# Deformable layer: one of eight corner products of a tap moved from ScalarE to GpSimd, behind a later tap's gathers

## The chip, the cores and the metric

The kernel runs on one core of one Trainium2 chip. The metric is the device time of one execution in microseconds (us), and the median of three runs stands for a kernel. The engines go by the names of the profile: PE is TensorE's matmul (PEld its weight load), DVE is VectorE, ACT is ScalarE, POOL is GpSimd, SP is SyncE, which here issues every transfer but the gathers.

## The reference

The input x has four images of 128 channels and 128 x 128 pixels. Each image goes through four layers, each a normalisation over groups of channels, a convolution of some kind and a residual sum. Layer 0, the one that matters here, is a deformable convolution. A 3 x 3 convolution gives, for each pixel and each of the nine taps, an offset in y and x and a mask. Each tap then reads the image at its own shifted, fractional position, by bilinear interpolation of the four pixels around it, and a 128 x 128 product with the tap's weights sums the nine taps:

```python
def corner(yi, xi, wgt):
    valid = (yi >= 0) & (yi < H) & (xi >= 0) & (xi < W)
    idx = jnp.clip(yi, 0, H - 1) * W + jnp.clip(xi, 0, W - 1)
    v = jax.vmap(lambda xb, ib: jnp.take(xb.reshape(C, H * W), ib, axis=1))(x, idx)
    return v * (wgt * valid)[:, None]
return corner(y0i, x0i, (1 - ly) * (1 - lx)) + corner(y0i, x0i + 1, (1 - ly) * lx) \
    + corner(y0i + 1, x0i, ly * (1 - lx)) + corner(y0i + 1, x0i + 1, ly * lx)
...
sampled = _bilinear_sample(x, py, px) * mask[:, None]
return jnp.einsum('bckhw,ock->bohw', sampled, weight.reshape(weight.shape[0], C, KK))
```

Layer 1 is a 5 x 7 dilated convolution. Layer 2 is a selective state-space block: its core is a scan with 16 states a channel over the pixels in four directions. Layer 3 is a 3 x 3 difference convolution.

## The kernel before

An image is cut into 32 blocks of four rows (512 pixels). In layer 0 a unit of work is a tap of a block: 32 x 9 = 288 taps an image, 1152 in all. Ahead of it, `layer0_table` writes the normalised image into a table in memory, in which one row holds the four pixels around a position, 4 x 128 numbers, so that one gathered row brings all that the interpolation of one output pixel needs. `positions` works out offsets, masks, indices (`idx`) and weights (`wt` for the two upper neighbours, a product in PSUM, `wl`, for the two lower ones) for strips of 16 rows.

A tap then goes through these steps:

- `gather` (L447): GpSimd issues four indirect DMAs, one for each row of the block, each of 128 table rows of 2 KB. Two rows share a tile `g` of 128 x (2 rows, 4 neighbours, 128 channels); so a tap has two tiles, h = 0 and h = 1. The partition is the pixel's column.
- `weigh_upper(h)` (L460): ScalarE multiplies the two upper neighbours of each of the tile's two rows by a column of `wt`, one instruction of 128 x 128 each, in place. That is four products a tile and eight a tap.
- `weigh_lower(h)` (L473): VectorE multiplies the lower neighbours of the tile's two rows by `wl`, one instruction of 128 x 512 a tile.
- `turn` (L484): TensorE transposes the 4 x 4 pieces and sums the four neighbours in PSUM, 16 matmuls with `ident`.
- `copy` (L496): ScalarE copies the 128 x 512 result out of PSUM into `smp`.
- `project` (L504): TensorE multiplies `smp` by the tap's weights and sums over the nine taps in `acc`.
- `add` (L511): after the ninth tap VectorE adds the residual.

The tiles of `g` come from a pool of `pairs` buffers: 20 for the first image, which is ten taps, and 10 for the others, which is five. A gather that needs a buffer waits until TensorE's `turn` of the tap that had it is done.

The order of instructions on each engine is the order in which the program writes them, and `keep_order` holds the compiler to it. `weave` sets that order: at step t it calls each stage of a list with the tap t minus the stage's delay, group after group.

```python
order = [[(2, weigh_upper(0)), (2, weigh_lower(0)), (3, turn), (5, project)], [(6, add), (0, gather), (4, copy(True))],
         [(2, weigh_upper(1)), (2, weigh_lower(1))], [(0, look), (3, copy(False))], []]
```

So at step t the gathers of tap t are written after the first half's products of tap t - 2 and before its second half's products. `look` advances `positions` of the next strip.

Layer 0 of the first image runs by itself. From then on `scan`, the core of layer 2, is the main work (`together`): after each step of the scan the program pulls pieces of side work, and layer 0 of the next image is a part of that. So layer 0 of images two, three and four is written between the scan's instructions. While it runs, `on_vector` gives the scan's two large products (L930, `inputs`, and L997, `outputs`) to VectorE and leaves on GpSimd only one product of 128 x 512 for each of the scan's blocks (L902), beside the gathers. VectorE also runs the scans themselves (L1073), for which ScalarE makes the decays (L960, `pa`), and TensorE spreads inputs (L923) and sums outputs (L971).

Of the kernel before, what the change touches and what calls it, by code (L numbers as in the profile page):

```python
# [13 lines left out]
AF = mybir.ActivationFunctionType  # L14
ALU = mybir.AluOpType
# [9 lines left out]
NBLK = H // R  # L25
KK = 9
# [86 lines left out]
def conv_preact_kernel(ctx: ExitStack, tc: tile.TileContext, a: dict, nb: int):  # L113
    nc = tc.nc
# [8 lines left out]
    def load(pool, src, shape, name, **kw):  # L123
        t = pool.tile(shape, F32, name=name, **kw)
        nc.sync.dma_start(t, src)
        return t
# [75 lines left out]
    def blk(t, i):  # L202
        return t[:, i * N : (i + 1) * N]
# [108 lines left out]
    def layer0(st, pairs=10):  # L312
# [5 lines left out]
        with ExitStack() as s:  # L318
# [8 lines left out]
            got = {}  # L327
# [106 lines left out]
            def where(n):  # L434
                i, k = divmod(n, KK)
                return i, k, i // BPS, i % BPS

            def gather(n):
                i, k, j, q = where(n)
                if k == 0:  # L440
                    got["x", i] = load(pp, blk(xb, i), [P, N], "xres", bufs=2)
                idx = got["i", j][1]
                for h in range(2):
                    got["g", n, h] = g = gp.tile([P, 2, 4, P], F32, name="g")
                    for r in range(2):
                        m = ((2 * h + r) * BPS + q) * KK + k
                        nc.gpsimd.indirect_dma_start(  # L447
                            out=g[:, r].rearrange("p q c -> p (q c)"),
                            out_offset=None,
                            in_=table,  # L450
                            in_offset=bass.IndirectOffsetOnAxis(ap=idx[:, m : m + 1], axis=0),
                        )

            def weigh_upper(h):
                def one(n):
                    i, k, j, q = where(n)
                    wv, g = got["i", j][0], got["g", n, h]
                    for r in range(2):
                        for c in range(2):
                            nc.scalar.activation(  # L460
                                g[:, r, c, :], g[:, r, c, :], AF.Copy, scale=wv[:, 2 * h + r, q, k, c : c + 1]
                            )

                return one

# [72 lines left out]
            for n, _ in enumerate(positions(0)):  # L538
                yield share * min(1.0, (n + 1) / 21)
            order = [[(2, weigh_upper(0)), (2, weigh_lower(0)), (3, turn), (5, project)], [(6, add), (0, gather), (4, copy(True))],  # L540
                     [(2, weigh_upper(1)), (2, weigh_lower(1))], [(0, look), (3, copy(False))], []]
            while st["rows"] <= NBLK:
# [841 lines left out]
    def head(b):  # L1384
        st = sts[b]
        table = [(loads(None, layer0_table(st), True), 12)] if b < 2 else []
        return table + [(loads("POOL", layer0(st)), 28), (loads("PE", layer1(st), True), 14),
                (loads("PE", layer2_pre(st), True), 36)]
# [11 lines left out]
    for f in layer0(sts[0], 20):  # L1400
        tick()
        for _ in range(3):
            next(ahead, None)
            tick()
# [103 lines left out]
```

## Time and profile before

| | us |
|---|---|
| median of three runs | 20858.84 (20851.53 to 20882.21) |
| the profiled execution | 20873.01 |
| its span, first to last instruction | 20871.2 |
| mean granted TensorE clock | 0.886 |

The profile is of one execution. Its times are in microseconds unless marked ns. A group's line gives the line of the kernel, the engine, the operation, tiles written and read, shapes, how many there are, busy time and mean ns of one, and then the engine's idle time just ahead of them with what ended it. The groups of layer 0's steps and of the scan's two large products:

| line | engine, what | count | busy us | mean ns |
|---|---|---|---|---|
| L447 | POOL, gathers | 4608 | 4807.6 | 1043 |
| L460 | ACT, upper neighbours | 9216 | 2897.4 | 392 |
| L473 | DVE, lower neighbours | 2304 | 1485.7 | 671 |
| L484 | PE, transposing matmuls | 18432 | 2693.6 | 303 |
| L496 | ACT, copies of PE's result | 1152 | 664.7 | 577 |
| L504 | PE, tap weights | 2304 | 1355.3 | 670 |
| L902 | POOL, 128x512 product of the scan's blocks | 512 | 652.9 | 1275 |
| L997 | DVE, 128x2048 product | 356 | 816.6 | 2294 |
| L997 | POOL, 128x2048 product | 1692 | 7670.8 | 4534 |

Idle time of an engine costs nothing unless others wait for it. "remote", or "another core or an unknown queue", marks a wait for which the profile names no instruction that ended it. "issue" is time in which the engine waited for nothing that the profile shows. A windows view gives the busy time of each engine in given stretches of the span. The chain of waits starts from what ended last and goes back, at each step, to what released it.

### The profile page before, as it was taken

How to read it: one execution, taken by the hardware profiler on the slowest of the kernel's cores; microseconds unless marked ns; L12 is line 12 of the kernel's file. 1: busy time of each engine (PE TensorE's matmuls, PEld its weight loads, DVE VectorE, ACT ScalarE, POOL GpSimd, SP SyncE). 2: the span in 40 equal slices, each digit the busy share in tenths (PEclk: the TensorE clock that was granted, in tenths of full speed). 3: DMA queues.
4: the chain of work that ended last, by engine and by line, in shares of the span. 5: the costliest groups of instructions: out<-in, count | busy, mean ns of one | idle time of the engine just before them, and what ended most of it. 6: DMA issues, size and time to landing. Idle time of an engine off the chain costs nothing.

```text
span 20871.2 us, 208527 instructions
## 1 busy us (share of the span) xinstructions
PE 15906.6 (76%) x58778; PEld 6786.0 (33%) x58778; DVE 16828.5 (81%) x14665; ACT 13184.7 (63%) x26230; POOL 15930.9 (76%) x9453
## 2 busy tenths in 40 slices
PE   4667776777878888777788887877777877677778
PEld 2444222444322223344422222344432222222223
DVE  1222588888999999878799889978889998999983
ACT  3444566677666666666667776666666767655563
POOL 3664577666788888777668888866768889999994
PEclk7878888889989999889889999988888988899899
DMA  7666678777767777777777796777776777555673
GB/s 234 191 193 190 193 228 284 248 255 252 246 206 226 231 237 254 236 253 255 247 232 226 224 249 230 255 240 246 252 237 218 235 215 220 185 185 193 199 219 120
DMA packets 2909344, 4717.42 MB, mean 226 GB/s; under 512 B 1095248, under 2 KB 1369240, under 8 KB 2831264
## 3 DMA queue, kind: packets, MB, share of 16 engines
q1 hardware_dynamic: 2539552, 3495.83, 52.3%
q0 software_dynamic: 368640, 1208.25, 18.5%
q8 instruction: 476, 7.80, 0.1%
q14 instruction: 676, 5.54, 0.1%
HBM read 3766.27 MB, written 908.60 MB: 224 GB/s over the span
## 4 chain that ended last, share of the span: by engine, by line
DVE 35%; PE 21%; issue 11%; ACT 11%; DMA 9%; another core or an unknown queue 5%; POOL 3%; SPq 3%; DVEq 0%; POOLq 0%; ACTq 0%
DVE h L1073 20%; DVE h L930 11%; PE pst L484 5%; PE psum L895 4%; DMA du<-stepsd 3%; ACT pa L960 3%; ACT g L460 3%; PE acc L504 2%; DVE g L473 2%; PE dub L923 2%; DMA delta<-stepsd 2%; PE yacc L971 2%; PE p L1303 1%; DMA g<-table,idx 1%
## 5 line engine op out<-in xcount | busy, mean ns | idle before, releaser
L1073 DVE TENSOR_TENSOR_SCAN h<-pa,carry,h 128x512 f32<-128x512 f32 x8192 | 10010.0, 1268 | 811.5 <-ACT pa L960 582.9
L960 ACT ACTIVATE pa<-delta,neg_a 128x512 f32<-128x512 f32 x8192 | 5535.9, 686 | 4528.0 <-DVE h L1073 3464.9
L997 POOL TENSOR_TENSOR h<-h,cb 128x2048 f32<-128x2048 f32 x1692 | 7670.8, 4534 | 136.3 <-POOL carry L991 0.4
L447 POOL DMA_INDIRECT g<-table,idx x4608 | 4807.6, 1043 | 2454.1 <-issue 1523.6
L930 DVE TENSOR_TENSOR h<-du,dub 128x2048 f32<-128x2048 f32 x1625 | 3688.0, 2270 | 961.8 <-PE dub L923 294.7
L484 PE MATMUL pst<-ident,g 128*128 128x128 f32 x18432 | 2693.6, 303 | 1242.6 <-issue 516.0
L923 PE MATMUL dub<-u,xb_sb 128*128 128x512 f32 x3250 | 2073.1, 724 | 1843.3 <-DVE h L930 1532.3
L484 PEld LDWEIGHTS pst<-ident,g 128*128 128x128 f32 x18432 | 2377.9, 158 | 2230.3 <-issue 1139.0
L460 ACT ACTIVATE g<-g,wt 128x128 f32<-128x128 f32 x9216 | 2897.4, 392 | 50.8 <-DMA g<-table,idx 47.6
L971 PE MATMUL yacc<-h,gather_sb 128*32 128x512 f32 x16384 | 2375.6, 644 | 108.9 <-POOL h L997 63.8
L930 POOL TENSOR_TENSOR h<-du,bb 128x2048 f32<-128x2048 f32 x423 | 1927.7, 4557 | 16.5 <-DMA du<-stepsd 16.5
L496 ACT COPY smp<-pst 128x512 f32<-128x512 f32 x1152 | 664.7, 577 | 1749.8 <-remote 1175.9
L473 DVE TENSOR_TENSOR g<-g,wl 128x512 f32<-128x512 f32 x2304 | 1485.7, 671 | 194.3 <-issue 108.5
L504 PE MATMUL acc<-smp,w_sb 128*128 128x512 f32 x2304 | 1355.3, 670 | 307.7 <-DVE x L511 162.8
L923 PEld LDWEIGHTS dub<-u,xb_sb 128*128 128x128 f32 x3250 | 600.3, 213 | 3025.2 <-DVE h L930 2200.9
L902 POOL TENSOR_TENSOR steps<-steps,u 128x512 f32<-128x512 f32 x512 | 652.9, 1275 | 1095.3 <-ACT steps L899 1080.0
L1303 PE MATMUL p<-xn,w_l_sb 128*128 128x508 f32 (+2 forms) x2304 | 1148.6, 620 | 1.8 <-ACT xn L1282 1.8
L971 PEld LDWEIGHTS yacc<-h,gather_sb 128*32 128x32 f32 x16384 | 343.5, 111 | 1886.3 <-issue 1349.6
L895 PE MATMUL psum<-e,ident 128*128 128x512 f32 x1024 | 607.1, 677 | 387.7 <-ACT bc L889 348.5
L511 DVE TENSOR_TENSOR x<-acc,xres 128x512 f32<-128x512 f32 x128 | 87.5, 684 | 967.5 <-remote 500.4
L895 PE MATMUL psum<-one_e,less 128*128 128x512 f32 x1024 | 629.2, 701 | 297.3 <-ACT one_e L891 296.5
L997 DVE TENSOR_TENSOR h<-h,cb 128x2048 f32<-128x2048 f32 x356 | 816.6, 2294 | 12.1
(169 smaller groups left out, 17288.9 us busy)
## 6 DMA issues: line engine op xcount, KB each, us to landing
cb<-bcd SPq DMA_DIRECT2D x512, 1024.0 KB
delta<-stepsd SPq DMA_DIRECT2D x2048, 256.0 KB
du<-stepsd SPq DMA_DIRECT2D x2048, 256.0 KB
stepsd<-steps SPq DMA_DIRECT2D x512, 512.0 KB
table<-gt SPq DMA_DIRECT2D x512, 256.0 KB
bb<-bcd SPq DMA_DIRECT2D x512, 256.0 KB
win<-nd SPq DMA_DIRECT2D x512, 160.0 KB
g<-table,idx POOLq DMA_INDIRECT x4608
```

Of the source, the lines that this page charges most:

```text
L447: nc.gpsimd.indirect_dma_start(out=g[:, r].rearrange("p q c -> p (q c)"), out_offset=None, in_=table, in_offset=bass.IndirectOffsetOnAxis( ...
L460: nc.scalar.activation(g[:, r, c, :], g[:, r, c, :], AF.Copy, scale=wv[:, 2 * h + r, q, k, c : c + 1])
L473: nc.vector.tensor_mul(g, g, wl.unsqueeze(3).to_broadcast([P, 2, 2, P]))
L484: nc.tensor.matmul(pst[:, r * P : (r + 1) * P], g[:, r % 2, q, :], ident, start=q == 0, stop=q == 3, is_transpose=True,)
L504: nc.tensor.matmul(got["a", i], w0[:, k, :], got.pop(("c", n)), start=k == 0, stop=k == KK - 1)
L895: nc.tensor.matmul(pd, sign, t, start=n == 0, stop=n == 3)
L923: nc.tensor.matmul(p, xb[:, seq[t][1], j, :], c["u"], start=True, stop=True)
L930: engine.tensor_mul(h, c["du"], b.unsqueeze(1).to_broadcast([P, NG, N]))
L960: nc.scalar.activation(pa, blocks[t]["d", g], AF.Exp, scale=neg_a[:, k, at : at + 1])
L971: nc.tensor.matmul(c["y"][g * Q : (g + 1) * Q, :], gather, c["h", j][:, g, :], start=j == 0, stop=last and not second,)
L997: engine.tensor_mul(h, h, c["cb"][:, j, :].unsqueeze(1).to_broadcast([P, NG, N]))
L1073: nc.vector.tensor_tensor_scan(o, f, o, carry[:, n : n + 1], ALU.mult, ALU.add)
```

## The change

At the end of `gather` of tap t, behind the last of its four indirect DMAs, GpSimd multiplies one upper neighbour of tap t - 2: of the second tile (h = 1), second row (r = 1), second neighbour (c = 1). ScalarE leaves that product out and keeps the other seven. The last two taps of an image have no tap two on, so ScalarE keeps all eight of them. A small function, `neighbour`, finds the piece and its weight for both engines. Nothing else differs.

```diff
                             in_offset=bass.IndirectOffsetOnAxis(ap=idx[:, m : m + 1], axis=0),
                         )
+                    if h == 1 and n >= 2:
+                        g, w = neighbour(n - 2, h, 1, 1)
+                        nc.gpsimd.tensor_scalar(g, g, w, None, ALU.mult)
+
+            def neighbour(n, h, r, c):
+                i, k, j, q = where(n)
+                return got["g", n, h][:, r, c, :], got["i", j][0][:, 2 * h + r, q, k, c : c + 1]
 
             def weigh_upper(h):
                 def one(n):
-                    i, k, j, q = where(n)
-                    wv, g = got["i", j][0], got["g", n, h]
                     for r in range(2):
                         for c in range(2):
-                            nc.scalar.activation(
-                                g[:, r, c, :], g[:, r, c, :], AF.Copy, scale=wv[:, 2 * h + r, q, k, c : c + 1]
-                            )
+                            if h == 1 and r == 1 and c == 1 and n + 2 < NBLK * KK:
+                                continue
+                            g, w = neighbour(n, h, r, c)
+                            nc.scalar.activation(g, g, AF.Copy, scale=w)
 
                 return one
```

## The prediction

> **What bounds the kernel now.** The change touches only the deformable layer, so I first looked for it in time. Of the views I read, in this order, the first is the page's first part, which shows no engine full over the span:
>
> ```profile
> PE 15906.6 (76%) x58778; PEld 6786.0 (33%) x58778; DVE 16828.5 (81%) x14665; ACT 13184.7 (63%) x26230; POOL 15930.9 (76%) x9453
> ```
>
> These are averages over unlike stages. The instructions of L447 (GpSimd's gathers) show that the layer runs four times, once an image, and one windows view gives the four stretches from first gather to last. Columns: stretch, its length, then busy us (and instructions) of PE, PEld, DVE, ACT, POOL, then clock, DMA share, GB/s.
>
> ```profile
> 215.00:1932.00 1717.00, 1026.82 (x5576) 738.58 (x5577) 431.75 (x751) 818.54 (x2541) 1091.61 (x1151) 0.79 0.64 191
> 3449.00:5327.00 1878.00, 1466.10 (x7295) 823.16 (x7295) 1624.06 (x1646) 1297.91 (x3361) 1278.10 (x1184) 0.89 0.75 251
> 8650.00:10449.00 1799.00, 1369.82 (x6976) 797.11 (x6976) 1416.08 (x1487) 1206.83 (x3207) 1267.88 (x1178) 0.88 0.76 248
> 13548.00:15368.00 1820.00, 1368.97 (x6966) 795.71 (x6967) 1415.21 (x1485) 1207.38 (x3208) 1273.85 (x1177) 0.87 0.75 245
> ```
>
> The reader is to see 7214 us, 35% of the span, in which ScalarE is busy 48%, 69%, 67% and 66%: not the fullest engine. POOL's busy time leaves something out. The timeline of POOL alone shows gathers 1.25 us apart, start to start, although each counts 0.95 us:
>
> ```profile
> 811.88 0.95 POOL L447 DMA_INDIRECT g<-table,idx  x1 [0.30 <-issue]
> 813.14 1.18 POOL L447 DMA_INDIRECT g<-table,idx  x1 [0.30 <-issue]
> 814.62 0.95 POOL L447 DMA_INDIRECT g<-table,idx  x1 [0.31 <-issue]
> 815.87 0.95 POOL L447 DMA_INDIRECT g<-table,idx  x1 [0.30 <-DVE g L473]
> ...
> 820.87 0.95 POOL L447 DMA_INDIRECT g<-table,idx  x1 [0.30 <-issue]
> 824.85 0.94 POOL L447 DMA_INDIRECT g<-table,idx  x1 [3.03 <-ACT smp L496]
> ```
>
> The 0.30 us ahead of a gather is there nearly every time (median over 4520 pairs 0.30). With 1152 x 0.30 = 346 us added, POOL is taken for 1438 of 1717, 1624 of 1878, 1614 of 1799 and 1620 of 1820 us: 84%, 86%, 90%, 89%. That leaves 279, 254, 185 and 200 us, 918 in all. A tap has four gathers, so POOL needs 5.0 us a tap at least; the taps come every 5.96, 6.52, 6.24 and 6.32 us.
>
> Next, who waits for whom in those gaps. ScalarE over the same microseconds:
>
> ```profile
> 809.74 2.45 ACT L460 ACTIVATE g<-g,wt 128x128 f32<-128x128 f32 x8
> 824.24 0.58 ACT L496 COPY smp<-pst 128x512 f32<-128x512 f32 x1 [12.04 <-remote]
> ```
>
> ScalarE's eight products take 2.45 us, far under the tap's 5.96; then it stands 12.04 us before a copy of PE's result. PE's last matmul of that copy's tap is recorded long before, yet PE's semaphore counts appear only at 824.1, 2.3 us after POOL had run out of gathers. In the first image 45 such releases of several counts at once come a median 2.07 us after POOL went idle. There POOL is also ten taps ahead of PE (its buffers' limit): turn follows landing by a median 43 us. So a round is: POOL works until its buffers are used up, goes idle some 2 to 3 us, PE's counts arrive, buffers come free. Its length is POOL's work plus a short idle; ScalarE's work lies inside it. I read POOL as the pacer in the first image, and as one of several in the other three, where DVE's scans (79% to 86% busy) run beside it.
>
> **The change, part by part.** For each tap but an image's last two, one of ScalarE's eight products moves: 286 an image, 1144 in all, ScalarE's L460 falls from 9216 to 8072.
>
> *Removed from ScalarE.* Eight take 2.45 us pipelined, so one is 0.30 us; 1144 of them 343 us of work. What of it was on the path: the chain of waits, asked for each stretch, gives "ACT g L460" 13.8%, 7.1%, 5.9% and 6.3%, that is 237 + 133 + 106 + 115 = 591 us; an eighth is 74 us. Where POOL paces, a shorter ScalarE ends nothing earlier, so I count a third: -25 us.
>
> *Added to POOL.* No 128x128 product with a column runs on POOL in this trace. From below: the one-input 128x128 select of masks.py:199 took 0.29 us. From above: two-input products took 1.275 us at 512 columns (L902) and 4.534 at 2048 (L997), 2.12 ns a column and 0.19 us fixed, so 0.46 us at 128; the farthest row, L902 itself, would be 1.27. I take 0.38, halfway between the near two, since it has one tensor input like the lower row but a scalar to fetch besides. Its neighbours matter as much:
>
> ```profile
> 9399.96 0.95 POOL L447 DMA_INDIRECT g<-table,idx  x1 [0.30 <-issue]
> 9400.93 1.27 POOL L902 TENSOR_TENSOR steps<-steps,u 128x512 f32<-128x512 f32 x1
> 9402.36 0.98 POOL L447 DMA_INDIRECT g<-table,idx  x1 [0.16 <-PE acc L504]
> ```
>
> A product behind a gather starts 0.02 us after it, and the next gather 0.16 us after the product. So the product costs 0.38 + 0.02 + 0.16 - 0.30 = 0.26 us of POOL's time (0.17 to 0.34 by the bounds): 74 us an image, 297 in all (194 to 389).
>
> *How much of it shows.* First image: all 74, since a round is POOL's work plus an idle that the change does not touch. Other three: POOL is taken 86% to 90%, rounds of the same kind but partly set by scans; I take two thirds of 223, 149 us. Together +223; if the idle 918 us covered it, nothing.
>
> *The new waits.* The product waits on POOL for the landing of a gather two taps back. Landing takes a median 3.7 us from issue, 7.4 at 95% and 10.1 at most; two taps back lies at least 5.0 us of gathers before. Behind a late one are queued the next tap's gathers, but POOL's instructions are accepted well before they run (at 815.5 a wait for the gather of 824.85 was already under way), so I cost it nothing; uncovered, a few tens of us. TensorE's turn waits for the product too, and VectorE's product of the lower half (L473), which today waits for ScalarE each time; the two touch interleaved rows of one tile. Today L473 of the second half starts a median 13.8, 5.3, 3.1 and 2.4 us after the end of the gathers two taps on, behind which the product will stand. Less than 0.8 us it is in 21%, 5%, 25% and 27% of the taps; in the last three images the shortfall is 0.09, 0.55 and 0.67 us a tap, 375 us if each counted. In the first image VectorE is 25% busy and it costs nothing. In the others a shortfall is a tap in which POOL is late, which the 149 us already has; I add none, and keep the 375 for a rival.
>
> *Moved past.* On POOL the product stands behind the fourth gather of its tap and ahead of the next tap's first; no DMA moves, SP's queue is untouched. L902, which feeds the scan, can stand 0.38 us later: 84 of them in these stretches, 32 us at most, within the range.
>
> **Sum.** +223 - 25 = +198 on the profiled execution's 20873.0 (span 20871.2 and 1.8 around it): 21071. The median of the three runs, 20858.8, is 14.2 lower, so 21057.
>
> **A rule weighed.** VectorE's two-input 128x2048 product stops POOL:
>
> ```profile
> 9221.97 2.29 DVE L997 TENSOR_TENSOR h<-h,cb 128x2048 f32<-128x2048 f32 x1
> 9222.25 2.84 POOL L447 DMA_INDIRECT g<-table,idx  x1 [0.30 <-issue]
> ```
>
> All 294 gathers of over 1.3 us overlap an L997, and none of the 84 L902 on POOL does. The Trainium skill (SBUF — State Buffer, Who interferes with whom) says that a VectorE instruction with two SBUF inputs blocks a GpSimd instruction that reads SBUF, but not one that only writes, descriptor generation included. The first half agrees with the L902 rows, the second does not agree with the 2.84 us gather. By the rule the products would be stopped on top of what is seen now; by the row POOL is stopped once by each L997 already, whichever instruction is next.
>
> **Rivals.**
> *The idle hides it (faster).* POOL fills its 918 us and the ScalarE share of the chain shrinks: -74, 20785. For it: in the last three images the chain gives POOL's gathers under 3% and ScalarE's products about 6%. Against: the idle comes after POOL's work, not beside it. Chance 0.24.
> *VectorE is held (slower, far).* Where VectorE catches up with POOL it stands for the product, and the scans behind it stand too. It decides once POOL's lead over VectorE falls under the product's 0.4 us, which a quarter of the taps of images three and four are near. All 297 and half of 375: +485, 21344. Chance 0.15.
> *Products stopped besides.* 334 L997 of 2.29 us in 5497 us: a product of 0.38 meets one in 16%, for some 1.15 us; 858 x 0.19 = 160 more, 21217. This is what that rule of the Trainium skill would make. For it: L902's rows; against: the stopped gathers. Chance 0.08.
> *The break frees PE's counts.* If the pause between gathers lets them through, the first image's 279 us of idle go, +74 stays: -205, 20654. Against: today's 0.30 us pauses, and L902's 1.27 us, release few. Chance 0.06.
> Forecast, POOL paces: 0.47, own range 20900 to 21190.
>
> **From cases to numbers.** 0.2% is 42 us, about what a measurement of this kernel can tell from no change. Faster: most of the first rival and the last, 0.25. Same: tails of forecast and first rival, 0.12. Slower 0.63. From 20740 to 21340 leaves out the last rival and half of the held one, some 0.15.
>
> **What would show it.** Right: the four stretches grow by about 74 and three times 50 us; POOL's new row is near 0.38 us, x1144, with gaps of 0.02 and 0.16; its idle stays near 918. Wrong: the idle shrinks by 297 and the stretches do not grow; or L473 waits for POOL in large sums; or a product of 0.6 us and more; or ScalarE's long waits for PE's counts grow rarer.

## The result and the profile after

The kernel after takes 20837.52 us (median of 18 runs, 20814.37 to 20856.60), the kernel before, measured beside it, 20880.28 us (18 runs, 20851.53 to 20901.91). The ratio is 0.9981, with a 95% interval from 0.9974 to 0.9988: **0.19% faster**, 43 us, where 0.9% slower was forecast. The profiled execution took 20838.75 us, its span 20837.0.

One thing must be said of the condition of these runs, since no later number can be understood without it: in this comparison PE's semaphore counts, by which it tells the other engines that a matmul is done, are recorded late and in bursts, as in the 12.04 us "remote" wait that the prediction shows, while in six of the eight groups of runs below they are on time and the same kernel before takes some 20,090 us.

The four stretches of layer 0 after the change, first gather to last, with columns as in the prediction's windows view (stretch, length, busy us of PE, PEld, DVE, ACT, POOL, clock, DMA share, GB/s):

```profile
217.00:1930.00 1713.00, 1048.80 (x5578) 748.18 (x5579) 434.35 (x751) 740.46 (x2264) 1288.72 (x1438) 0.80 0.64 191
3446.00:5309.00 1863.00, 1434.60 (x7314) 805.93 (x7313) 1645.09 (x1654) 1227.41 (x3092) 1540.28 (x1470) 0.90 0.78 254
8625.00:10444.00 1819.00, 1356.92 (x7011) 772.64 (x7011) 1439.83 (x1497) 1147.39 (x2946) 1489.62 (x1464) 0.90 0.76 246
13536.00:15357.00 1821.00, 1373.55 (x7011) 781.71 (x7011) 1436.60 (x1500) 1147.43 (x2946) 1490.43 (x1464) 0.89 0.76 246
```

The lengths make 7216 us; before they made 7214. POOL's busy time rose by 898 us, ScalarE's fell by 268, and the stretches did not move. The page's groups, with line numbers shifted (L460 became L468), give the cost:

```profile
L447 POOL DMA_INDIRECT g<-table,idx x4608 | 4874.2, 1058 | 1679.5 <-issue 1136.4
...
L468 ACT ACTIVATE g<-g,wt 128x128 f32<-128x128 f32 x8072 | 2577.6, 392 | 216.7 <-DMA g<-table,idx 162.4
...
L455 POOL TENSOR_SCALAR g<-g,wt 128x128 f32<-128x128 f32 x1144 | 833.0, 728 | 37.4
```

The product is far longer than the 0.38 us forecast: 0.728 us in the mean, 0.624 in the median. POOL's timeline shows how it stands between gathers, once where the buffers are used up in the first image, once in the third:

```profile
821.10 0.95 POOL L447 DMA_INDIRECT g<-table,idx  x1 [0.30 <-issue]
822.08 0.62 POOL L455 TENSOR_SCALAR g<-g,wt 128x128 f32<-128x128 f32 x1
824.79 1.05 POOL L447 DMA_INDIRECT g<-table,idx  x1 [2.09 <-issue]
...
9398.72 0.95 POOL L447 DMA_INDIRECT g<-table,idx  x1 [0.30 <-issue]
9399.70 0.76 POOL L455 TENSOR_SCALAR g<-g,wt 128x128 f32<-128x128 f32 x1
9400.64 1.01 POOL L447 DMA_INDIRECT g<-table,idx  x1 [0.17 <-issue]
```

In the median it starts 0.03 us after the fourth gather, the next gather follows 0.17 us behind it, and that gather takes 1.01 us instead of 0.95. So a product costs POOL 0.62 + 0.03 + 0.17 + 0.06 - 0.30 = **0.58 us** a tap, against 0.26 in the forecast. With 0.30 us added for each of 866 gathers and 0.20 for each of 286 products in a stretch (317 us), POOL is taken for all but 107, 6, 12 and 14 us: its idle is 139 us, where it was 918. The work did not make the stretches longer; it filled the idle.

### The profile page after: what moved, and what is told of

The parts are those of the page before. It is cut to its first block, busy times and chain, and to the rows that moved or that the text cites. A ratio compares the mean times of both kernels' runs of the same rounds, so it can differ in the third digit from the quotient of the medians.

```text
span 20837.0 us, 209864 instructions
## 1 busy us (share of the span) xinstructions
PE 15847.0 (76%) x58778; PEld 6719.5 (32%) x58778; DVE 16855.7 (81%) x14665; ACT 12887.2 (62%) x25086; POOL 16827.5 (81%) x10597
## 4 chain that ended last, share of the span: by engine, by line
DVE 34%; PE 19%; issue 12%; DMA 11%; ACT 10%; POOL 8%; another core or an unknown queue 3%; SPq 2%; DVEq 0%; POOLq 0%; ACTq 0%
DVE h L1079 20%; DVE h L936 11%; PE pst L490 4%; PE psum L901 4%; POOL g L447 3%; DMA du<-stepsd 3%; ACT pa L966 3%; DMA g<-table,idx 2%; PE acc L510 2%; ACT g L468 2%; DMA delta<-stepsd 2%; PE p L1309 1%; POOL h L1003 1%; PE yacc L977 1%
## 5 line engine op out<-in xcount | busy, mean ns | idle before, releaser
L1003 POOL TENSOR_TENSOR h<-h,cb 128x2048 f32<-128x2048 f32 x1692 | 7670.5, 4533 | 137.0 <-POOL carry L997 0.6
L447 POOL DMA_INDIRECT g<-table,idx x4608 | 4874.2, 1058 | 1679.5 <-issue 1136.4
L490 PEld LDWEIGHTS pst<-ident,g 128*128 128x128 f32 x18432 | 2312.0, 155 | 2699.8 <-issue 1297.6
L468 ACT ACTIVATE g<-g,wt 128x128 f32<-128x128 f32 x8072 | 2577.6, 392 | 216.7 <-DMA g<-table,idx 162.4
L479 DVE TENSOR_TENSOR g<-g,wl 128x512 f32<-128x512 f32 x2304 | 1488.2, 669 | 359.9 <-DMA g<-table,idx 315.4
L455 POOL TENSOR_SCALAR g<-g,wt 128x128 f32<-128x128 f32 x1144 | 833.0, 728 | 37.4
```

Source lines behind the costliest of these rows:

```text
L447: nc.gpsimd.indirect_dma_start(out=g[:, r].rearrange("p q c -> p (q c)"), out_offset=None, in_=table, in_offset=bass.IndirectOffsetOnAxis( ...
L468: nc.scalar.activation(g, g, AF.Copy, scale=w)
L479: nc.vector.tensor_mul(g, g, wl.unsqueeze(3).to_broadcast([P, 2, 2, P]))
L490: nc.tensor.matmul(pst[:, r * P : (r + 1) * P], g[:, r % 2, q, :], ident, start=q == 0, stop=q == 3, is_transpose=True,)
L1003: engine.tensor_mul(h, h, c["cb"][:, j, :].unsqueeze(1).to_broadcast([P, NG, N]))
```

## The experiments

Eight groups of runs were made; in a group each kernel is compared with the kernel before on one chip. Each kernel has one trace in its group, and whether counts are late was read from it: by ScalarE's waits "ACT smp <- remote", and by stalls, spans of over 2 us between two recorded counts of PE in which at least two of its matmuls that count have their recorded ends; a stall's length is the time from the last such end to the next count. In the kernels with ScalarE relieved and no real product on GpSimd (e1, e3, g1, h3) one upper neighbour goes unweighted into the sum.

| group | counts | before, us | kernels |
|---|---|---|---|
| first comparison | late | 20880.28 | after |
| 1 | on time | 20088.11 | e1, e2, e3, e4 |
| 2 | on time | 20108.61 | c0, c1, c2, c3 |
| 3 | on time | 20091.91 | d1 |
| 4 | on time | 20098.10 | d2 |
| 5 | late | 20863.10 | f1, f2 |
| 6 | on time | 20092.19 | g1, g2, g3 |
| 7 | on time | 20085.07 | h1 |
| 8 | late | 20879.30 | h2, h3 |

### The two halves of the change, each alone, and a doubled one

e1 is the kernel after without GpSimd's product; ScalarE keeps seven. e2 is the kernel before, ScalarE with all eight, and a product of the same size on a tile of its own (`scratch`, by a column of -1) in the product's place. e3 is the kernel after with that scratch product instead of the real one, so that nobody waits for it. e4 gives GpSimd two products a tap and ScalarE six.

e1, against the kernel after:

```diff
-                    if h == 1 and n >= 2:
-                        g, w = neighbour(n - 2, h, 1, 1)
-                        nc.gpsimd.tensor_scalar(g, g, w, None, ALU.mult)
```

e2, against the kernel before (e3 has the same product, against the kernel after, in place of the real one):

```diff
+                    if h == 1 and n >= 2:
+                        nc.gpsimd.tensor_scalar(scratch, scratch, minus, None, ALU.mult)
```

e4, against the kernel after:

```diff
-                        g, w = neighbour(n - 2, h, 1, 1)
-                        nc.gpsimd.tensor_scalar(g, g, w, None, ALU.mult)
+                        for c in range(2):
+                            g, w = neighbour(n - 2, h, 1, c)
+                            nc.gpsimd.tensor_scalar(g, g, w, None, ALU.mult)
...
-                            if h == 1 and r == 1 and c == 1 and n + 2 < NBLK * KK:
+                            if h == 1 and r == 1 and n + 2 < NBLK * KK:
```

> The eighth product is left out: ScalarE does seven, GpSimd none, so one upper neighbour goes into the sum unweighted. Theory S (slack: GpSimd's idle time before the change was spare, and ScalarE's product is a small part of the path): 0.2 to 0.5% faster than before, 20780 to 20840 us, since an eighth of ScalarE's 591 us on the chain is 74 us at most. Theory C (cancel: both engines are on the path, the changed kernel gains much on ScalarE and pays much on GpSimd): 1 to 3% faster, 20250 to 20670 us. The forecast's theory (GpSimd paces): within 0.1%, since a shorter ScalarE ends nothing earlier.

> ScalarE does all eight products as before; GpSimd does a product of the same size on a scratch tile at the same place, with no data of the tap. Theory S: within 0.3% of before (20820 to 20940), GpSimd's idle in images two to four falls from some 200 us to under 30 us each. Theory C: 1 to 3% slower (21090 to 21500). GpSimd paces: 1144 products of 0.57 us are 650 us, 21400 to 21530.

> ScalarE does seven, GpSimd a product of the same size on a scratch tile: the changed kernel's work on each engine without the wait of TensorE on GpSimd (the eighth neighbour stays unweighted). In the changed kernel TensorE's turns wait some 500 us for GpSimd's product. If that wait costs, this run is faster than the changed kernel by 0.2% or more (under 20800); if it only takes the place of waits for ScalarE and transfers, both are the same within 0.1% (20820 to 20860). Theory C expects the same as the changed kernel, 20840.

> Two of the eight products on GpSimd (both neighbours of the second tile's second row), six on ScalarE. Theory S: GpSimd is already full in images two to four (5 to 11 us idle), so each tap there pays the second product in full: 858 x 0.6 to 0.7 us = 510 to 600 us, and image one, with 98 us idle, pays some 65 us: 21400 to 21500. Theory C: the second product gains on ScalarE what it costs on GpSimd: within 0.3% of the changed kernel.

| kernel | us | ratio to before (95%) |
|---|---|---|
| e1, ScalarE relieved | 20071.31 | 0.9991 (0.9982 to 1.0000) |
| e2, GpSimd loaded | 20710.61 | 1.0304 (1.0290 to 1.0318) |
| e3, both, nobody waits | 20692.30 | 1.0300 (1.0286 to 1.0314) |
| e4, two products | 21336.07 | 1.0623 (1.0607 to 1.0639) |

Here the product is no gain but 3% of the kernel, and two are 6.2%. The kernel before was 790 us faster than in the first comparison. Either these kernels differ from the change in something not yet seen, or the group differs.

### The same two kernels once more, and a break without work

c0 is the kernel before, c1 the kernel after, both unedited, and c2 is e2 again. c3 puts a memset of one column into the kernel before, in the place of the product:

```diff
+                    if h == 1 and n >= 2:
+                        nc.gpsimd.memset(tiny, 0.0)
```

> The kernel before, unchanged, for a profile beside the others of its group. The first group's chip ran it in 20088 us, the chip of the first comparison in 20880. Theory H (held counts): the 790 us lie in the four stretches of layer 0, and a chip's time goes with how many of PE's counts appear late in bursts there: near 20090 with none, near 20880 with some 200. Theory K (another cause, such as slower transfers or a lower clock): the stretches outside layer 0 differ as well.

> The changed kernel, unchanged. On a chip without late counts GpSimd paces: 3.0% slower than before, 20680 to 20720 us, since the same work with a scratch tile took 20692 and 20711. On a chip with late counts: 0.1 to 0.3% faster than before, some 20840, as in the first comparison. If it is 0.2% faster on a chip whose before takes 20090, the data wait of the scratch runs was misread.

> ScalarE eight products, GpSimd one besides on a scratch tile. Where counts come late: GpSimd's 1144 products fill the idle that the late counts leave, so within 0.3% of before, about 20850 to 20940; if instead ScalarE's relief made the changed kernel's gain, it is slower than the changed kernel by 74 us or more. Where they don't: 3% slower, 20710.

> ScalarE eight products; GpSimd only clears one column of 128 x 1 behind each tap's gathers (some 0.1 us). If any other instruction between the gathers lets PE's counts through, a chip with late counts gains up to 600 us or so (20200 to 20400). If the counts need a pause in the gathers, or GpSimd's work only fills idle time, it stays within 0.3% of before there. Where no counts come late: 0 to 0.4% slower, 1144 x 0.04 us = 46.

c0 took 20102.89 us (0.9998, 0.9989 to 1.0008), c1 **20690.66 (1.0293, 1.0279 to 1.0307)**, c2 20717.45 (1.0302, 1.0287 to 1.0318), c3 20106.66 (1.0002, 0.9993 to 1.0011). So it is the group: the very kernel that gained 0.19% loses 2.9% where counts are on time. The first and third image of c0, the kernel before with counts on time:

```profile
217.00:1663.00 1446.00, 1001.89 (x5693) 660.76 (x5694) 483.30 (x762) 912.76 (x2597) 1091.99 (x1152) 0.92 0.76 227
...
8227.00:9875.00 1648.00, 1323.36 (x7016) 772.88 (x7016) 1433.49 (x1497) 1222.91 (x3226) 1293.87 (x1178) 0.91 0.83 272
```

POOL's busy 1091.99 and 346 us of gaps fill 1438 of 1446 us: no idle is left. Its timeline in the first image is gather after gather, 1.25 us apart, without the 3 us holes of the prediction's fence:

```profile
1007.85 0.95 POOL L447 DMA_INDIRECT g<-table,idx  x1 [0.30 <-issue]
1009.10 0.95 POOL L447 DMA_INDIRECT g<-table,idx  x1 [0.30 <-issue]
1010.36 0.95 POOL L447 DMA_INDIRECT g<-table,idx  x1 [0.30 <-issue]
```

The same two images of c1, the kernel after:

```profile
218.00:1832.00 1614.00, 1023.03 (x5671) 680.16 (x5671) 483.66 (x763) 801.18 (x2313) 1292.28 (x1438) 0.90 0.69 203
...
8512.00:10319.00 1807.00, 1360.95 (x7007) 770.38 (x7008) 1437.05 (x1497) 1151.38 (x2945) 1483.59 (x1463) 0.90 0.77 248
```

The first grows by 168 us, 0.587 a tap, and the third by 159, 0.556: close to the 0.58 us that the timeline gave for a product. All four stretches go from 6486 to 7079 us, +593, where the medians of c1 and c0 lie 588 apart. The waits of c1, with columns of sum, count and longest in us, show PE now standing for the product:

```profile
PEld pst L490 <- POOL g L455: 1829.7, 838, 7.8
PE pst L490 <- POOL g L455: 1626.7, 815, 7.4
```

Yet e3, in which nobody waits for it, costs as much (1.0300 against 1.0293). The price is POOL's time, not the wait. The memset of c3 takes 0.118 us of POOL and costs nothing: it fits into the 0.30 us that stand ahead of a gather anyway, and the gathers on either side of it start 1.25 us apart as before.

### Less work on POOL: a shorter product, and none of L902

d1 is the kernel before with L902 given to VectorE while layer 0 runs beside the scan:

```diff
-            nc.gpsimd.tensor_mul(du, delta, u)
+            (nc.vector if early else nc.gpsimd).tensor_mul(du, delta, u)
```

d2 is e2 with 48 of 128 columns:

```diff
-                        nc.gpsimd.tensor_scalar(scratch, scratch, minus, None, ALU.mult)
+                        nc.gpsimd.tensor_scalar(scratch[:, 0:48], scratch[:, 0:48], minus, None, ALU.mult)
```

> The kernel before, with the scan's product of 128 x 512 (du) on VectorE instead of GpSimd while layer 0 runs beside the scan: 84 times 1.27 us of GpSimd less, 84 times some 0.68 us of VectorE more. If GpSimd paces images two to four (no late counts), each product that goes takes 1.27 + 0.02 + 0.15 - 0.30 = 1.14 us off, 96 us in all, less what VectorE loses waiting in order for ScalarE's steps: 0.2 to 0.5% faster. If VectorE's scans pace, 0.1 to 0.4% slower. If PE's late counts pace (the first comparison's chip), within 0.2%.

> ScalarE eight products; GpSimd one besides on 48 of the scratch tile's 128 columns. The full product took 0.624 us and cost 0.54 us a tap where no counts come late; a cleared column of some 0.1 us cost nothing. If the cost is duration less a fixed 0.1 us that the next gather's own 0.30 us of preparation hides, a product of 0.3 to 0.4 us costs 0.2 to 0.3 us a tap, 230 to 340 us, 1.1 to 1.7%. If instead any read of SBUF by GpSimd costs the same, whatever its length, 2.5 to 3%. On a chip with late counts: within 0.3% of before.

d1 took 20039.65 us, **0.9974 (0.9964 to 0.9984)**, and its stretches 6432 us, 54 fewer than c0's: taking work off POOL gains, where counts are on time. d2 took 20481.17 us, 1.0191 (1.0177 to 1.0205). The product's rows in c1 and d2 (shortest, median and longest in ns):

```profile
L455 POOL TENSOR_SCALAR g<-g,wt x1144: 619/626/2788, 232.6 to 15204.4; 128x128 f32<-128x128 f32 x191
```

```profile
L456 POOL TENSOR_SCALAR scratch<-scratch,minus x1144: 419/426/2577, 232.3 to 14994.8; 128x48 f32<-128x48 f32 x191
```

Eighty columns are 0.200 us, 2.5 ns a column, and 0.626 - 128 x 0.0025 = 0.31 us is fixed. d2's first image grows by 105 us over c0's, 0.37 us a tap.

### The product beside an engine that is later than POOL

f1 and f2 are before and after with matmuls added at the head of each `turn`, 22 in the first image and 10 in the others, whose result is overwritten: PE is then the pacer.

```diff
+                for _ in range(22 if pairs == 20 else 10):
+                    nc.tensor.matmul(pst[:, 0:P], ident, ident, start=True, stop=True)
```

> The kernel before, with TensorE made slower: each tap's turn starts with 22 (first image) or 10 (the others) redundant matmuls of the identity into the same bank, some 2.7 and 1.2 us a tap, which the real ones overwrite. It stands in for a chip on which something other than GpSimd paces layer 0. 2 to 5% slower than before on any chip; GpSimd's idle in the four stretches rises from some 100 us to several hundred.

> The changed kernel with the same redundant matmuls. If GpSimd's product is free as long as GpSimd has idle time (the theory of the first comparison's chip), this takes the same as the kernel before with the slow TensorE, within 0.5%, although without them the changed kernel is 2.9% slower than before. If the product costs its 0.54 us a tap beside any pacer, or through the wait of TensorE for it, it is 2 to 3% slower than that.

f1 took 21909.3 us, 1.0500 (1.0482 to 1.0517), f2 21912.77, 1.0501 (1.0483 to 1.0518). The first image of f1:

```profile
216.00:2453.00 2237.00, 2189.30 (x17798) 1973.11 (x17799) 429.27 (x751) 825.28 (x2536) 1100.75 (x1152) 0.99 0.50 147
```

and of f2:

```profile
216.00:2456.00 2240.00, 2187.03 (x17804) 1973.72 (x17805) 430.86 (x751) 743.58 (x2256) 1293.12 (x1438) 0.99 0.50 147
```

PE is busy 98% of either; POOL's idle goes from 790 to 630 us in the first image and from 1905 to 1198 in all four, and the stretches from 8200 to 8218. Behind another pacer the product is free, and ScalarE's relief is worth nothing. This group is one of those with late counts, yet in f1's first image, where POOL is idle 35% of the time, a single count comes late, by 24 us at its very start, and none after.

### Meeting late counts with the halves

g1 and h3 are e1 again, g2, h1 and h2 are e2 again, g3 is c3 again. Three groups were spent on it; only the last had late counts.

> The eighth product left out, nothing on GpSimd. On a chip with late counts (before near 20870): if ScalarE's relief makes the gain of the changed kernel, 0.2 to 0.5% faster than before; if GpSimd's product itself changes the late counts, within 0.1% of before. On a chip without: 0.1% faster, as before.

> ScalarE eight, GpSimd one besides on a scratch tile. On a chip with late counts: within 0.3% of before, if GpSimd's work fills idle time there; faster by 0.2% or more would mean that its product shortens the late counts by more than it costs; 0.4% slower or more would mean that the relief of ScalarE is what balances it in the changed kernel. On a chip without: 3.0% slower.

> ScalarE eight, GpSimd clears one column of 128 x 1 behind each tap's gathers. On a chip with late counts: within 0.2% of before if only GpSimd's time matters; 1 to 3% faster if any other instruction between the gathers lets PE's counts through. On a chip without: the same as before.

> ScalarE eight products, GpSimd one besides on a scratch tile. On a chip with late counts (before near 20870): within 0.3% of before if GpSimd's work fills idle time; 0.4% slower or more if the relief of ScalarE balances it in the changed kernel; faster by 0.2% or more if the product shortens the late counts by more than it costs. On a chip without (before near 20090): 3.0% slower, for the third time.

> ScalarE eight products, GpSimd one besides on a scratch tile. Late counts (before near 20870): within 0.3% of before if GpSimd's work fills idle time; 0.4% slower or more if ScalarE's relief balances it in the changed kernel. No late counts (before near 20090): 3.0% slower.

> ScalarE seven products, the eighth left out. Late counts: 0.2 to 0.5% faster than before if ScalarE's relief makes the changed kernel's gain, within 0.1% if not. No late counts: 0.1% faster.

| kernel | counts | us | ratio to before (95%) |
|---|---|---|---|
| g1, ScalarE relieved | on time | 20073.88 | 0.9992 (0.9982 to 1.0001) |
| g2, GpSimd loaded | on time | 20709.18 | 1.0307 (1.0289 to 1.0324) |
| g3, memset | on time | 20098.16 | 0.9999 (0.9989 to 1.0009) |
| h1, GpSimd loaded | on time | 20701.72 | 1.0306 (1.0286 to 1.0327) |
| h2, GpSimd loaded | late | **20829.99** | **0.9978 (0.9968 to 0.9988)** |
| h3, ScalarE relieved | late | 20845.40 | 0.9985 (0.9976 to 0.9995) |

h2 does more work than the kernel before, nothing less, and is faster. Its first and third image:

```profile
218.00:1928.00 1710.00, 1059.69 (x5567) 749.15 (x5568) 433.79 (x751) 819.04 (x2536) 1291.86 (x1438) 0.80 0.66 192
...
8619.00:10441.00 1822.00, 1388.59 (x7016) 802.79 (x7016) 1443.40 (x1500) 1237.01 (x3230) 1496.23 (x1463) 0.88 0.77 246
```

This is the picture of the kernel after, without ScalarE's relief. All in one table: lengths of the four stretches, POOL's idle in them, and the stalls of late counts.

| kernel | counts | stretches, us | POOL idle, us | stalls, us | over 4 us |
|---|---|---|---|---|---|
| before | late | 7214 | 918 | 953 | 46 |
| after | late | 7216 | 139 | 612 | 9 |
| h2, GpSimd loaded | late | 7213 | 124 | 622 | 15 |
| h3, ScalarE relieved | late | 7188 | 883 | 968 | 54 |
| c0, before | on time | 6486 | 96 | 0 | 0 |
| c1, after | on time | 7079 | 22 | 0 | 0 |

With late counts the kernel before takes 728 us more in its stretches than c0, and POOL's idle is 822 us more. The product fills most of that. A slower PE does not explain the 728: the granted clock is lower (0.79 against 0.92 in the first image), but PE's busy time in the four stretches is 5232 us against 5046, only 186 more. ScalarE's waits for late counts, of which c0 and c1 have none, shrink too; of the kernel before and then of the kernel after:

```profile
ACT smp L496 <- remote: 1175.9, 219, 34.3
```

```profile
ACT smp L502 <- remote: 1013.2, 200, 27.9
```

**What stays open.** Why counts come late at all, and why in some groups: the runs of a group agree in their times, and groups 5 and 7, one late and one on time, carry the same chip number in the record, so if that number names one chip, the condition is not fixed to it. Since the ends of matmuls are modelled, the traces do not tell either whether the count is late or the matmul.

Why the product makes the stalls shorter is open as well. Bursts of three counts and more, recorded within 0.1 us of each other, all fall in a pause of POOL: 76 in the first image of before, 1.0 to 3.2 us after the end of its last gather, and 50 in that of after, 1.1 to 2.1 us after it, 47 of these with the product as POOL's last work. The one late count of f1's first image is recorded 6.3 us after the end of its opening gathers, which follow one another without a pause. This fits counts that come through when GpSimd pauses its gathers. Against it, 12 of the 60 stalls of over 2 us in the first image of before, and 18 of the 30 in that of after, end while a gather runs. So it is not shown. The memset of c3 and g3, which would have tried a pause without work, met late counts in neither group, and d1 was not tried with them.

Nor are the 43 us located. Measured from the first gather to the last, not by whole microseconds, the stretches sum to 7216.8 us before and 7215.0 after, and the rest of the span goes from 13,654 to 13,622. In h2, h3, c0 and c1 that rest is 13,608 to 13,623, so before's one profile stands out, and a single profile can't say whether by chance. The two halves' gains, 0.22% and 0.15%, do not add up to the whole, 0.19%.

No kernel here is shown to beat both under both conditions. d1 beats them where counts are on time, after and h2 beat the kernel before where they are late.

## Why the prediction was wrong

**The step that failed** is "a round is POOL's work plus an idle that the change does not touch". It was drawn from a trace in which that idle goes with PE's late counts (c0, without them, has 96 us of it), and the change touched it first: 918 us of idle became 139, POOL's work with its gaps rose by some 780, and the stretches did not grow. The prediction had the row in hand (the release 2.3 us after POOL ran out) and read the order "POOL stops, then counts come" as a fixed pause. Its line on what would show it wrong, "the idle shrinks by 297 and the stretches do not grow", is what the trace shows, with 779 for the 297.

**"POOL paces"** is right where counts are on time: c0 has 96 us of idle, and +593 us comes from POOL's time alone (e2, e3, e4, d2 scale with it, d1 goes below). With the counts late it is not the pacer, though its taken share of 84% to 90% looked like it.

**The product** was mis-sized: 0.62 us, outside the bounds of 0.29 and 0.46; neither the select nor the two-input row has the fixed 0.31 us and the 2.5 ns a column of this form. The net of 0.26 should have been 0.58, and for the four images 593 us by c1 instead of 297. The gaps of 0.02 and 0.16 held nearly (0.03 and 0.17); the gather behind takes 0.06 more, which was not foreseen. The Trainium skill (GPSIMD Engine Reference, 3.1 Elementwise — side-by-side cycle accounting) gives a best case of 1.8 cycles an element at 1.2 GHz, by which a column would take an estimated 1.5 ns; the rows of c1 and d2 have 2.5.

**ScalarE's relief**, -25 us, held: -0.09% (17 us, e1) and -0.08% (18 us, g1), intervals that reach to no change or just about, and -0.15% with late counts (h3).

**The waits cost nothing** held. VectorE's L479 waits for the product 0.5 us in all, so the rival "VectorE is held" is out; PE waits 497.5 and 549.6 us in the kernel after, and e3 shows that this sets nothing.

**Products stopped besides**: 73 of the 1144 products last over 0.85 us, 66 of them beside VectorE's two-input L1003, and add 116 us to POOL. With counts on time the gathers are stopped that much less (what gathers of over 1.05 us last beyond 0.95 goes from 525 us in c0 to 446 in c1, and the products' 81 fill the difference), as the prediction read its 2.84 us gather. With late counts the gathers' share stayed (444 and 439 us). The Trainium skill (SBUF — State Buffer, Who interferes with whom) has a VectorE instruction with two SBUF inputs contend with a GpSimd instruction that reads SBUF, over ports that it calls an exclusive lock; the rows agree from the other side too, as 13 of the 356 L1003 on VectorE last over 2.4 us, up to 3.98, all beside a product, while the median is 2.29 and before the change none lasts over 2.36.

**The rivals that came nearest** are "The idle hides it" and "The break frees PE's counts". The first has the effect right, but it gave ScalarE's share as the gain, and h2 shows that this share is not needed: it keeps ScalarE's eight products and gains as much. The second has the stalls grow rarer as they did, 46 long ones down to 9, but it wanted 205 us in the first image, which gained 4.

## What to carry to other kernels

An idle that follows an engine's work each round is not part of that engine's cost until it is known what ends it: ask what releases the engine, and whether added work would run inside the same wait. Before a small gain is believed, run the kernel before again in another group of runs; here the same change is 0.19% faster or 2.9% slower, by a condition that shows in the time of the kernel before and in the waits for PE's counts. An engine that a view shows 76% busy (POOL in c0's first image) can be full: add the gap ahead of each of its instructions before work is moved to it.

## What the runs showed of the hardware

- PE's counts can be recorded late after the matmul's recorded end, in the trace of before by 1 to 10 us in 268 stalls and by over 10 in three, in some groups of runs and not in others. In such groups the kernel before takes 3.9% longer (20,880 against 20,090 us).
- A one-input 128x128 product with a column as scalar takes GpSimd 0.626 us (c1), by the 48 columns of d2 2.5 ns a column and 0.31 fixed: more a column than its two-input products (2.12 ns by L902 and L997).
- Gathers of 128 rows of 2 KB go out at best every 1.25 us, of which 0.30 is not counted as busy; an instruction of 0.12 us fits into that gap for nothing (c3: gathers still 1.25 us apart over it).
